# Fetch order of row names, buffers of three weight matrices, and the order of a product and a pair of transposes in a four-layer graph network

## Chip, cores and metric

The kernel runs on one core of a Trainium2 chip, as one launch. The metric is the device time of that launch in microseconds; smaller is better. Everything is in float32.

## The reference, cut to what matters

Four layers follow each other. Each one adds a graph layer over 2708 nodes of 256 features and then a feed-forward layer with routed experts to `x`. The change touches the second half of layer 1 and the start of layer 2:

```python
# layer 1, feed-forward: a shared hidden layer, then one of 8 matrices per row
H = gelu(layernorm(x) @ W1 + b1)               # 2708 x 1024
probs = softmax(H @ Wg + bg);  assign = argmax(probs)
for e in range(8):
    out += where(assign == e, probs[:, e] * (H @ Wd[e] + bd[e]), 0)
x = x + out
# layer 2, graph attention
h = layernorm(x) @ W.T
a_src = (h * attn_src).sum(-1);  a_dst = (h * attn_dst).sum(-1)
s = leaky_relu(a_src[None, :] + a_dst[:, None], 0.2), masked by adj > 0
x = x + elu(softmax(s) @ h)
```

## The kernel before

**Tiles.** Rows are worked on in 22 tiles of 128 rows (the last one has 20). `x` stays in SBUF for the whole program. The five engines are PE (matrix products and transposes), DVE and ACT (element-wise), POOL (which also starts the indirect DMAs) and SP (which starts the plain DMAs). Each engine works through its own queue in order; the framework places the waits between them and may arrange instructions of independent steps within a queue. `engine_after`, `after` and `in_order` pin an order by hand.

**Layer 1, second half.** While the graph product of a group of tiles ends, `send1` computes the hidden layer of the group and its gates, writes the hidden rows to DRAM (`hid`, line 1267) and scatters a short record for each row (its index and its weight, `taken1`, line 537), sorted by expert. Then the rows are taken up again in blocks of 128 rows that share one expert. Nine blocks (`NA`) are certain: the first two groups fill them whatever the routing of the third. Fifteen more (`ALWAYS`) take the rest.

The class `Units` runs the blocks. For a block it needs

- the names: 128 records, gathered by POOL (`fetch_names`, line 551 by way of `gather`),
- the rows: 128 hidden rows of 4 KB, gathered by POOL by those names into one of four buffers `hs` (`fetch_rows`, line 693),
- the expert's matrix, 1152 KB, loaded by SP (`weights1`, line 1170); the load is left out when the buffer already holds this expert.

PE then transposes the rows (`turn`, line 708, copied to `hTs` by ACT at line 709), multiplies (`output`, line 781), DVE adds the bias and scales (lines 784 and 785), and POOL scatters the result to DRAM (`given1`, line 537). `more` is called once per block and decides what is fetched ahead: as many rows as there are buffers, one block of names beyond that (three once all nine certain blocks have their rows), and two matrices.

**Buffers of the matrices.** `buffer_of` gives each block a buffer. The certain blocks go round three of them, in the order 0, 3, 6, 1, 4, 7, 2, 5, 8 of the sorted blocks (`in_thirds`), so that neighbours with one expert meet in one buffer. Three more lie where the gates of `send1` had their tiles (pool `w1r`, opened when the gates are closed). The rest's blocks follow the list `REST1` of (block, buffer). Ahead of block 18 stands a branch on a count that comes out as zero here (`branch`); its body recomputes blocks that hold more rows than planned.

**The turn to layer 2.** The results of tiles 0 to 7 (`EARLY`) are read back and added to `x` while the last blocks still run (line 1485); their statistics for the first two of `FOURS` (tiles 0 and 1, tiles 2 to 5) are made there too. The tiles from 8 on can be added only after the last block's scatter. Layer 2 starts by going over `FOURS`: `turned_up` adds the results (line 1587; by DVE up to tile 13, by POOL from tile 14 on) and transposes (line 1592, copied by ACT at line 1594), `valued` multiplies by the weights with two score columns (line 267), ACT takes the scores (line 1629) and exponentials, and DVE writes the scaled values (line 1632). `row_scores` and `row_factor` spread the scores over all partitions. Two of `FOURS` are prepared ahead. The third, tiles 6 to 9, is half early and half late: `finish` adds and transposes the late tiles 8 and 9 in the middle of the second four's products,

```python
if i == 2 and ahead and callable(ahead[0][2]):
    ahead[0] = (*ahead[0][:2], ahead[0][2]())
ps.append(times(xT, k, r, w_l2, D + 2, ps_acc()))
```

so that on PE two products come first, then the late transposes, then the other two products. `ps_acc` goes round five PSUM banks here, `ps_tmp` round three.

Of the kernel before, what the change touches and what calls it, by code (L numbers as in the profile page):

```python
# [8 lines left out]
F32 = mybir.dt.float32  # L9
# [57 lines left out]
def adj_ffn4(ctx: ExitStack, tc: tile.TileContext, a: dict, out: bass.AP):  # L67
# [594 lines left out]
    class Units(Blocks):  # L662
# [59 lines left out]
        def more(self, weights=True):  # L722
            while self.rows_todo and len(self.rows) < len(self.hs):
                if not self.named:
                    self.fetch_names(self.names_todo.pop(0))
                self.fetch_rows()
                self.rows_todo -= 1
            while self.names_todo and len(self.named) < (3 if self.places[1] >= self.border else 1):
                self.fetch_names(self.names_todo.pop(0))
            while weights and self.todo and len(self.ahead) < 2:  # L730
                self.fetch(self.todo.pop(0))
            if weights and not self.todo:
                self.fetch_rest()
# [142 lines left out]
    with ExitStack() as l0:  # L876
# [261 lines left out]
    ALWAYS, AHEAD1 = 15, 9  # L1138
    EARLY, prepared = GROUPS1[0], {}

    REST1 = [(0, 3), (4, 4), (6, 2), (1, 3), (5, 4), (7, 2), (2, 3), (8, 2), (3, 3),
             (9, 5), (10, 1), (11, 4), (12, 0), (14, 2), (13, 0)]

    def buffer_of(b):

        return b % 3 if b < NA else REST1[b - NA][1]

    assert sorted(b for b, _ in REST1) == list(range(ALWAYS))
    assert all(b < AHEAD1 for b, _ in REST1[:AHEAD1])
    with ExitStack() as l1:  # L1150
# [179 lines left out]
        def beside(b):  # L1330
            if b == NA + AHEAD1 + 1:
                work1.at_end = scattered["given1"][-1].name
            if b in (NA + ALWAYS - 3, NA + ALWAYS - 2):
                first = len(nc.cur_bb.bb.instructions)
                for t0 in EARLY[::2][(b - NA - ALWAYS + 3) * 2 :][:2]:
                    add_early(t0)
                engine_after(first, mybir.EngineType.DVE, work1.last)
            if b == NA + ALWAYS - 1:
                for some in FOURS[:2]:
                    prepared[some[0]] = stats(some, by_log=True)[1]  # L1340
            if b == NA + 4:
# [123 lines left out]
        def branch():  # L1465

            with tc.If(left[0] > 0):
# [48 lines left out]
    with tc.tile_pool(name="t3", reuse_waits="tile", bufs=1) as t3:  # L1516
# [34 lines left out]
        with tc.tile_pool(name="g2", reuse_waits="tile", bufs=1) as gp:  # L1551
# [17 lines left out]
            def turned_up(tiles):  # L1569

                n, t0 = len(tiles), tiles[0]
                adder = v if t0 < FOURS[4][0] else g
                xT = gp.tile([P, DC, W], F32, name="xT4", bufs=2)
                late = [t for t in tiles if t not in EARLY]
                if late:
                    o = gp.tile([P, 4, D], F32, name="mine", bufs=2)
                    for i in load_tiles(nc, o, late, given[1], t0):
                        behind(i, scattered["given1"])

                def two(k):  # L1580
                    r = rows(t0 + k + 1)
                    for q, m in (((P, 2),) if r == P else ((P, 1), (r, 1))):
                        i = k if q == P else k + 1
                        if t0 + i in EARLY:
                            continue
                        xs = x[:q, t0 + i : t0 + i + m, :]
                        adder.tensor_tensor(xs, xs, o[:q, i : i + m, :], ALU.add)
                    p = ps_tmp()
                    for i in range(2):
                        q = rows(t0 + k + i)  # L1590
                        for c in range(DC):
                            te.transpose(p[:, (c * 2 + i) * P : (c * 2 + i) * P + q],
                                         x[:q, t0 + k + i, c * P : (c + 1) * P], ident[:q, :q])
                    s.copy(xT[:, :, k * P : (k + 1) * P + r],
                           p.rearrange("p (c t) -> p c t", c=DC)[:, :, : P + r])

                def scale():
                    return prepared[t0] if t0 in prepared else stats(tiles, by_log=True)[1]

                if len(late) in (0, n):  # L1600
                    for k in range(0, n, 2):
                        two(k)
                    return tiles, xT, scale()
                for k in range(0, n - len(late), 2):
                    two(k)

                def finish():
                    had, first = last_of(fronts), len(nc.cur_bb.bb.instructions)
                    had[mybir.EngineType.DVE] = last_put[0]
                    for k in range(n - len(late), n, 2):  # L1610
                        two(k)
                    for e in fronts:
                        engine_after(first, e, had[e])
                    return None

                return tiles, xT, finish

            def valued(tiles, xT, rstd):

                n, t0 = len(tiles), tiles[0]  # L1620
                own = tiles_of(t0 * P, (n - 1) * P + rows(tiles[-1]))
                sc = gp.tile([P, 4, 2], F32, name="sc", bufs=2)
                (v if tiles in FOURS[:2] else g).memset(sc, 0.0)
                ps = []
                for i, (t, k, r) in enumerate(own):
                    if i == 2 and ahead and callable(ahead[0][2]):
                        ahead[0] = (*ahead[0][:2], ahead[0][2]())
                    ps.append(times(xT, k, r, w_l2, D + 2, ps_acc()))
                    s.activation(sc[:r, i, :], ps[-1][:, D:], AF.Copy, scale=rstd[:r, i : i + 1])
                lnexp(hh[:, t0 : t0 + n, D], sc[:, :n, 0], AF.Exp)  # L1630
                for i, (p, (t, k, r)) in enumerate(zip(ps, own)):
                    put = v.tensor_scalar(hh[:r, t, :D], p[:, :D], rstd[:r, i : i + 1],
                                          hh[:r, t, D :], op0=ALU.mult, op1=ALU.mult)
                last_put[:] = [put.ins.name]
                lnexp(G[:, t0 : t0 + n, 0], sc[:, :n, 0], AF.Exp, scale=-0.8)

                lnexp(rowe[:, t0 : t0 + n, 0], sc[:, :n, 1], AF.Exp, scale=-0.2, bias=ln8)
                return sc, t0, n

            ahead, todo = [turned_up(FOURS[0])], list(FOURS[1:])  # L1640
            for k in range(len(FOURS)):
                tiles, xT, rstd = ahead.pop(0)
                sc, t0, n = valued(tiles, xT, rstd)
                if ahead and ahead[0][2] is None:
                    ahead[0] = (*ahead[0][:2], stats(ahead[0][0], by_log=True)[1])
                had, first = {}, len(nc.cur_bb.bb.instructions)
                while todo and len(ahead) < 2:
# [640 lines left out]
```

## Time and profile before

| | us |
|---|---|
| median of 3 runs | 1890.63 (1887.06 to 1890.68) |
| the profiled execution's own time | 1905.2 |
| its span, first to last instruction | 1903.5 |
| PE busy in the span | 1822.0 |
| DVE, ACT, POOL busy | 1074.7, 656.6, 388.5 |
| blocks of layer 1, first transpose to last product | 958.7 to 1090.6 |
| first transposes of layer 2 to its first attention product | 1090.4 to 1118.9 |

The profile was taken of one execution, and its times are counted from the start of its span. A line of a timeline gives the start, the length, the engine, the line of the kernel, the operation, what is written and read, and how many instructions were merged; in brackets stands how long the engine was idle before it and what ended that. A wait's line gives who waited for whom: microseconds in total, how many times, and the longest. PE's products of float32 are recorded as two instructions each with 128-column weights. The kind "DMA_INDIRECT" on POOL is the making of the descriptors; the data land later.

### The profile page before, as it was taken

The numbers are of one execution on the slowest core, as the hardware profiler recorded it, in microseconds if no ns is written. First come the engines' busy times: TensorE is split into PE (matmuls) and PEld (weight loads), VectorE is DVE, ScalarE is ACT, GpSimd is POOL, SyncE is SP. The second block draws the span as 40 slices with busy tenths as digits, with TensorE's granted clock in tenths as the row PEclk, the third lists the DMA queues.
The fourth block names the chain that finished last, engine by engine and source line by source line (L and its number), as shares of the span: only waits on it lengthen the run. The fifth ranks groups of instructions, "written<-read, shape, count | busy, mean of one in ns | idle before, by whom it ended". The sixth has DMA issues, their size and how long they took to land. (4 is left out here: it accounts for less than half of the span.)

```text
span 1903.5 us, 25846 instructions
## 1 busy us (share of the span) xinstructions
PE 1822.0 (96%) x9453; PEld 1333.3 (70%) x9453; DVE 1074.7 (56%) x2467; ACT 656.6 (34%) x1472; POOL 388.5 (20%) x460
## 2 busy tenths in 40 slices
PE   8999998999998999999988999999899999999998
PEld 7888777888887888878777878888566733233344
DVE  7687862443433625354542265555355398888877
ACT  8877741222222302113222232222232552132232
POOL 0014353333322001403446410000000100011021
PEclk9999999999999999999999999999899999999999
DMA  8535655887773554544746541000101000012020
GB/s 263 156 105 164 227 184 212 328 330 274 284 286 105 180 153 123 128 128 129 213 139 213 172 93 20 1 1 1 44 1 34 17 1 23 23 26 37 23 37 18
DMA packets 92638, 232.81 MB, mean 122 GB/s; under 512 B 18223, under 2 KB 48983, under 8 KB 84952
## 3 DMA queue, kind: packets, MB, share of 16 engines
q1 hardware_dynamic: 70936, 184.46, 29.8%
q0 software_dynamic: 21568, 46.61, 9.0%
q8 instruction: 78, 1.28, 0.3%
q14 instruction: 56, 0.46, 0.1%
HBM read 218.39 MB, written 30.80 MB: 131 GB/s over the span
## 5 line engine op out<-in xcount | busy, mean ns | idle before, releaser
L2160 DVE SCALAR_TENSOR_TENSOR e<-arena,G,mask 128x1024 f32<-128x1024 f32 (+1 forms) x252 | 275.0, 1149 | 34.2 <-PE den L2197 33.2
L2189 PE MATMUL num<-e,wh 128*64 128x512 f32 (+4 forms) x1056 | 214.0, 549 | 0.7 <-ACT L_gnn_W L1498 0.3
L1420 PE MATMUL acc<-sup,adrow 128*128 128x256 f32 x882 | 199.9, 384 | 3.1 <-DVE adrow L1388 1.7
L1024 PE MATMUL acc<-msg,wt 128*128 128x256 f32 x882 | 199.1, 382 | 2.7 <-DVE wt L974 2.0
L1723 PE MATMUL ps_acc<-hh,e 128*128 128x257 f32 x882 | 199.2, 382 | 1.7 <-ACT o L1666 1.7
L1420 PEld LDWEIGHTS acc<-sup,adrow 128*128 128x128 f32 x882 | 166.2, 191 | 31.3 <-issue 5.5
L1024 PEld LDWEIGHTS acc<-msg,wt 128*128 128x128 f32 x882 | 165.9, 191 | 29.0 <-DVE wt L974 3.0
L1723 PEld LDWEIGHTS ps_acc<-hh,e 128*128 128x128 f32 x882 | 163.7, 190 | 29.2 <-ACT o L1666 4.2
L649 PE MATMUL yacc<-wb,hTs 128*128 128x256 f32 x736 | 170.9, 384 | 5.6 <-DVE ys L651 2.9
L615 PE MATMUL ps_acc<-xTs,wa 128*128 128x256 f32 (+1 forms) x768 | 170.3, 374 | 4.6 <-DVE xTs L605 2.6
L617 ACT ACTIVATE hTs<-ps_acc,wa 128x256 f32<-128x256 f32 (+1 forms) x192 | 88.7, 465 | 246.7 <-PE yacc L649 165.5
L615 PEld LDWEIGHTS ps_acc<-xTs,wa 128*128 128x128 f32 x768 | 136.9, 190 | 31.6 <-DVE xTs L605 5.7
L2189 PEld LDWEIGHTS num<-e,wh 128*64 128x64 f32 (+1 forms) x1056 | 70.0, 136 | 122.8 <-issue 105.0
L649 PEld LDWEIGHTS yacc<-wb,hTs 128*128 128x128 f32 x736 | 138.4, 192 | 24.9 <-DVE ys L651 4.0
L1715 DVE SCALAR_TENSOR_TENSOR e<-Rb,G,mask 128x640 f32<-128x640 f32 (+2 forms) x110 | 84.9, 773 | 90.6 <-PE ps_acc L1723 90.5
L2197 PE MATMUL den<-e,wh 128*32 128x512 f32 (+4 forms) x1056 | 112.2, 545 | 0.0
L1385 DVE TENSOR_SCALAR mask<-adrow 128x1024 uint8<-128x1024 f32 (+1 forms) x66 | 41.4, 627 | 123.8 <-DMA adrow<-in_adjT 123.2
L221 ACT COPY xT<-ps_tmp 128x256 f32<-128x256 f32 x76 | 26.8, 366 | 199.6 <-PE ps_tmp L220 199.1
L781 PE MATMUL yacc<-wb,hTs 128*128 128x256 f32 x384 | 90.9, 392 | 0.0
L974 DVE SCALAR_TENSOR_TENSOR wt<-adrow,wt 128x640 f32<-128x640 f32 (+3 forms) x67 | 71.1, 1063 | 25.7 <-ACT wt L141 24.0
L2197 PEld LDWEIGHTS den<-e,wh 128*32 128x32 f32 (+1 forms) x1056 | 33.0, 109 | 73.7 <-issue 69.6
L537 POOL DMA_INDIRECT given<-ys,xs x46 | 65.4, 1421 | 91.2 <-DVE ys L652 76.9
(487 smaller groups left out, 2626.0 us busy)
## 6 DMA issues: line engine op xcount, KB each, us to landing
adhalf<-in_adjT SPq DMA_DIRECT2D x42, 677.0 KB
wb<-in_L_ffn_W2p SPq DMA_DIRECT2D x24, 1152.0 KB
wb<-in_L_ffn_Wdp SPq DMA_DIRECT2D x24, 1152.0 KB
wa<-in_L_ffn_W1b SPq DMA_DIRECT2D x24, 1028.0 KB
adrow<-in_adjT SPq DMA_DIRECT2D x42, 512.0 KB
adrow<-in_adjT SPq DMA_DIRECT2D x42, 320.0 KB
adrow<-in_adjT SPq DMA_DIRECT2D x21, 576.0 KB
adrow<-in_adjT SPq DMA_DIRECT2D x21, 448.0 KB
```

The source lines that it names most:

```text
L615: i = te.matmul(p[:, f % 2, : m * P], lhsT=w1[:, c, f * P : (f + 1) * P], rhs=xT[:, c, : m * P], start=(c == 0), stop=(c == DC - 1))
L617: s.activation(hT[:, f, : m * P], p[:, f % 2, : m * P], AF.Gelu, bias=bias[:, f : f + 1])
L649: te.matmul(q[:, k, :], lhsT=hT[:, f, k * P : (k + 1) * P], rhs=w2[:, f, :], start=(f == 0), stop=(f == HC - 1))
L781: te.matmul(q, lhsT=hT[:, f, :], rhs=w2[:, f, :], start=(f == 0), stop=(f == HC - 1))
L974: v.scalar_tensor_tensor(wt, ad, 1.0, wt, op0=ALU.is_lt, op1=ALU.mult)
L1024: te.matmul(p[:q, n - pair[0], :], lhsT=wt[:, k : k + q], rhs=msg[:r, j, :], start=(j == 0 and n == pair[0]), stop=(j == FULL - 1 and n == ...
L1420: te.matmul(p[:q, n - pair[0], :], lhsT=ad[:, k : k + q], rhs=sup[:, jj, :], start=(jj == 0 and n == pair[0]), stop=(jj == FULL - 1 and n ...
L1715: i = v.scalar_tensor_tensor(e[:r, :w], Rb[:r, c0 : c0 + w], G[:r, j, :], mask[:r, j, c0 : c0 + w], op0=ALU.max, op1=ALU.mult)
L1723: te.matmul(p[:, : D + 1], lhsT=e[:, k : k + q], rhs=hh[:, j, :], start=(j == 0), stop=False)
L2160: v.scalar_tensor_tensor(e[:, :w], slow[:, m % 2, k, :w], G[:, j, 2 * pair + k, :], mask[:, j, c0 : c0 + w], op0=ALU.max, op1=ALU.mult)
L2189: te.matmul(num[k * DK : (k + 1) * DK, hf, :q], lhsT=wh[some, j, 2 * pair + k, :DK], rhs=e[some, :q], start=(j == 0), stop=(j == FULL), ti ...
L2197: te.matmul(den[z * Q : (z + 1) * Q, :q], lhsT=wh[some, i, 2 * pair + k, DK : DK + 1] .to_broadcast([some.stop - some.start, Q]), rhs=e[so ...
```

## The change

It has four parts.

1. `more` fetches the names of all nine certain blocks in a row, behind the first three blocks' rows, instead of one block ahead. For the rest nothing changes (up to three ahead, once the ninth block's rows are on their way).
2. `buffer_of`: the last three of the nine certain blocks (in running order 6, 7, 8) get the buffers 3, 4, 5 in the gates' room instead of 0, 1, 2. `REST1` is renamed to match: 3 becomes 0, 4 becomes 1, 2 becomes 5, 5 becomes 2, 1 becomes 4, 0 becomes 3. The branch uses buffer 0 instead of 3.
3. The statistics of tiles 6 and 7 are made beside the last two blocks, with those of tiles 0 to 5.
4. `finish` is split. `add_late` adds tiles 8 and 9 on DVE at the place where `finish` stood. The second four's products run through; then the product of tile 6 (`begin_values` up to 1), then the transposes of tiles 8 and 9 (`turn_late`), their statistics, and the products of tiles 7 to 9.

```diff
-            while self.names_todo and len(self.named) < (3 if self.places[1] >= self.border else 1):
+            while self.names_todo and (self.places[0] < self.border or
+                                       self.places[1] >= self.border and len(self.named) < 3):
                 self.fetch_names(self.names_todo.pop(0))
...
-    REST1 = [(0, 3), (4, 4), (6, 2), (1, 3), (5, 4), (7, 2), (2, 3), (8, 2), (3, 3),
-             (9, 5), (10, 1), (11, 4), (12, 0), (14, 2), (13, 0)]
+    REST1 = [(0, 0), (4, 1), (6, 5), (1, 0), (5, 1), (7, 5), (2, 0), (8, 5), (3, 0),
+             (9, 2), (10, 4), (11, 1), (12, 3), (14, 5), (13, 3)]
...
-        return b % 3 if b < NA else REST1[b - NA][1]
+        return (b % 3 if b < NA - 3 else b - NA + 6) if b < NA else REST1[b - NA][1]
...
             if b == NA + ALWAYS - 1:
-                for some in FOURS[:2]:
+                for some in (*FOURS[:2], [t for t in FOURS[2] if t in EARLY]):
                     prepared[some[0]] = stats(some, by_log=True)[1]
...
-                work1.all_again(hc, items[AHEAD1:], wbs[3][0],
+                work1.all_again(hc, items[AHEAD1:], wbs[0][0],
                                 slice(NA + AHEAD1, NA + ALWAYS))
             pin(scattered["given1"][-1].name)
-            wbs[3][1] = None
+            wbs[0][1] = None
...
-                def finish():
+                def add_late():
+                    first = len(nc.cur_bb.bb.instructions)
+                    for k in range(n - len(late), n, 2):
+                        add_two(k)
+                    engine_after(first, mybir.EngineType.DVE, last_put[0])
+
+                def turn_late():
                     had, first = last_of(fronts), len(nc.cur_bb.bb.instructions)
-                    had[mybir.EngineType.DVE] = last_put[0]
                     for k in range(n - len(late), n, 2):
-                        two(k)
+                        turn_two(k)
                     for e in fronts:
                         engine_after(first, e, had[e])
...
+            def begin_values(tiles, xT, rstd, sc, ps, upto):
+                own = tiles_of(tiles[0] * P, (len(tiles) - 1) * P + rows(tiles[-1]))
+                while len(ps) < upto:
+                    i = len(ps)
+                    t, k, r = own[i]
+                    if i == 2 and ahead and type(ahead[0][2]) is tuple:
+                        ahead[0][2][1]()
+                    ps.append(times(xT, k, r, w_l2, D + 2, ps_acc()))
+                    s.activation(sc[:r, i, :], ps[-1][:, D:], AF.Copy, scale=rstd(i, r))
+                return own
...
-                if ahead and ahead[0][2] is None:
-                    ahead[0] = (*ahead[0][:2], stats(ahead[0][0], by_log=True)[1])
                 had, first = {}, len(nc.cur_bb.bb.instructions)
+                if ahead and type(ahead[0][2]) is tuple:
+                    tiles, xT, (m, _, turn_late) = ahead[0]
+                    some = prepared[tiles[0]]
+                    begun = scores_of(tiles)
+                    begin_values(tiles, xT, lambda i, r: some[:r, i : i + 1], *begun, 1)
+                    turn_late()
+                    first = len(nc.cur_bb.bb.instructions)
+                    others = stats(tiles[m:], by_log=True)[1]
+                    engine_after(first, mybir.EngineType.DVE, last_put[0])
...
+                    ahead[0] = (tiles, xT, rstd, begun)
+                    begin_values(tiles, xT, rstd, *begun, len(tiles))
+                    had, first = last_of(fronts), len(nc.cur_bb.bb.instructions)
```

Outside the lines shown, `two` is split into `add_two` and `turn_two`, `valued` into `scores_of`, `begin_values` and the rest, and the scale is passed as a function of the tile.

More of the change, by code (lines that the diff above doesn't have):

```diff
@@ L1578, in turned_up, with add_two @@
                         behind(i, scattered["given1"])
-                def two(k):
+                def add_two(k):
                     r = rows(t0 + k + 1)
@@ L1587, in two, with turn_two @@
                         adder.tensor_tensor(xs, xs, o[:q, i : i + m, :], ALU.add)
+                def turn_two(k):
+                    r = rows(t0 + k + 1)
                     p = ps_tmp()
@@ L1598, in scale @@
                     return prepared[t0] if t0 in prepared else stats(tiles, by_log=True)[1]
+                for k in range(0, n if len(late) == n else n - len(late), 2):
+                    add_two(k)
+                    turn_two(k)
                 if len(late) in (0, n):
-                    for k in range(0, n, 2):
-                        two(k)
-                    return tiles, xT, scale()
-                for k in range(0, n - len(late), 2):
-                    two(k)
-                def finish():
+                    rstd = scale()
+                    return tiles, xT, lambda i, r: rstd[:r, i : i + 1]
@@ L1608, in finish @@
+                def add_late():
+                    first = len(nc.cur_bb.bb.instructions)
+                    for k in range(n - len(late), n, 2):
+                        add_two(k)
+                    engine_after(first, mybir.EngineType.DVE, last_put[0])
+                def turn_late():
                     had, first = last_of(fronts), len(nc.cur_bb.bb.instructions)
-                    had[mybir.EngineType.DVE] = last_put[0]
                     for k in range(n - len(late), n, 2):
-                        two(k)
+                        turn_two(k)
@@ L1612, in finish @@
                     for e in fronts:
                         engine_after(first, e, had[e])
-                    return None
-                return tiles, xT, finish
-            def valued(tiles, xT, rstd):
-                n, t0 = len(tiles), tiles[0]
[L1621 to L1629, printed above, removed]
+                return tiles, xT, (n - len(late), add_late, turn_late)
@@ new lines, in scores_of @@
+            def scores_of(tiles):
+                sc = gp.tile([P, 4, 2], F32, name="sc", bufs=2)
+                (v if tiles[0] < FOURS[2][0] else g).memset(sc, 0.0)
+                return sc, []
+            def begin_values(tiles, xT, rstd, sc, ps, upto):
[8 more added lines that the diff above has]
+                return own
@@ L1630, in valued @@
+            def valued(tiles, xT, rstd, begun=None):
+                n, t0 = len(tiles), tiles[0]
+                sc, ps = begun or scores_of(tiles)
+                own = begin_values(tiles, xT, rstd, sc, ps, n)
                 lnexp(hh[:, t0 : t0 + n, D], sc[:, :n, 0], AF.Exp)
                 for i, (p, (t, k, r)) in enumerate(zip(ps, own)):
-                    put = v.tensor_scalar(hh[:r, t, :D], p[:, :D], rstd[:r, i : i + 1],
-                                          hh[:r, t, D :], op0=ALU.mult, op1=ALU.mult)
+                    put = v.tensor_scalar(hh[:r, t, :D], p[:, :D], rstd(i, r), hh[:r, t, D :],
+                                          op0=ALU.mult, op1=ALU.mult)
@@ L1641, in adj_ffn4, with rstd @@
             for k in range(len(FOURS)):
-                tiles, xT, rstd = ahead.pop(0)
-                sc, t0, n = valued(tiles, xT, rstd)
-                if ahead and ahead[0][2] is None:
-                    ahead[0] = (*ahead[0][:2], stats(ahead[0][0], by_log=True)[1])
+                sc, t0, n = valued(*ahead.pop(0))
                 had, first = {}, len(nc.cur_bb.bb.instructions)
+                if ahead and type(ahead[0][2]) is tuple:
[7 more added lines that the diff above has]
+                    engine_after(first, mybir.EngineType.DVE, last_put[0])
+                    def rstd(i, r):
+                        return some[:r, i : i + 1] if i < m else others[:r, i - m : i - m + 1]
+                    ahead[0] = (tiles, xT, rstd, begun)
+                    begin_values(tiles, xT, rstd, *begun, len(tiles))
+                    had, first = last_of(fronts), len(nc.cur_bb.bb.instructions)
                 while todo and len(ahead) < 2:
```

## The prediction, made before the changed kernel was run

> **What bounds the kernel now.** I read the page first, then PE's waits, then the busy time by stage over layer 1's second half (the stage that the change touches), then the timelines of PE, POOL and SP there. TensorE is busy for 96% of the span, so an edit can win only where PE stands still, or where it runs slowly after standing still.
>
> ```profile
> PE 1822.0 (96%) x9453; PEld 1333.3 (70%) x9453; DVE 1074.7 (56%) x2467; ACT 656.6 (34%) x1472; POOL 388.5 (20%) x460
> ```
>
> Four of PE's longer single waits in the whole program lie inside the 160 us concerned (total, times, longest):
>
> ```profile
> PE ps_acc L708 <- ACT hTs L709: 6.9, 1, 6.9
> ...
> PE ps_acc L708 <- PEq L1467: 3.6, 1, 3.6
> ...
> PE ps_acc L708 <- DMA hs<-hid,names: 3.3, 1, 3.3
> ...
> PE ps_tmp L1592 <- DVE x L1587: 2.4, 1, 2.4
> ```
>
> By stage (PE busy, PEld, DVE, ACT, POOL, clock, DMA share, GB/s): PE loses 6.7 of 17 us with the DMA engines mostly idle, then 4.5 of 23 us with them full. POOL is the busiest after PE.
>
> ```profile
> 978.00:995.00 17.00, 10.28 (x46) 9.13 (x47) 3.79 (x17) 2.83 (x5) 9.87 (x10) 0.80 0.32 94
> 995.00:1018.00 23.00, 18.51 (x97) 15.84 (x96) 2.71 (x7) 3.92 (x7) 14.49 (x15) 0.95 0.94 360
> ```
>
> Call the stalls A (977.8 to 984.7) and B (1011.7 to 1016.7). Timeline lines of both:
>
> ```profile
> 984.08 1.07 ACT L709 COPY hTs<-ps_acc 128x512 f32<-128x512 f32 x2 [10.35 <-remote]
> ...
> 984.72 1.97 PE L708 MATMUL ps_acc<-ident,hs 128*128 128x128 f32 x8 [6.95 <-ACT hTs L709]
> ...
> 1003.27 1.04 POOL L693 DMA_INDIRECT hs<-hid,names  x1 [0.30 <-PE ps_acc L708]
> ...
> 1015.05 0.63 PE L708 MATMUL ps_acc<-ident,hs 128*128 128x128 f32 x4 [3.35 <-DMA hs<-hid,names]
> ...
> 1016.70 1.11 PE L708 MATMUL ps_acc<-ident,hs 128*128 128x128 f32 x4 [1.02 <-issue]
> 1017.60 6.05 PE L781 MATMUL yacc<-wb,hTs 128*128 128x256 f32 x16
> ```
>
> B is read directly: counted in order, the gather of hidden rows issued at 1003.27 is the eleventh, and PE's eleventh set of turns waits until 1015.05 for it, 11.8 us. A gather with idle DMA engines (issued 965.50) has its last packet at 969.6: 4.1 us. Stall A ends on a copy of ACT whose own releaser the trace does not show ("remote"); DVE's and SP's instructions are held in the same microseconds. I can't name its cause.
>
> What holds the gathers back is on POOL's queue and SP's:
>
> ```profile
> 961.39 1.00 POOL L551 DMA_INDIRECT names<-taken,b_ix  x1 [0.31 <-issue]
> ...
> 965.50 1.04 POOL L693 DMA_INDIRECT hs<-hid,names  x1 [3.11 <-DMA names<-taken,b_ix]
> ...
> 991.54 0.37 SPq L1170 DMA_DIRECT2D wb<-in_L_ffn_Wdp  x1
> 994.99 5.14 SPq L1170 DMA_DIRECT2D wb<-in_L_ffn_Wdp  x3
> ```
>
> The names of one block are fetched only one block ahead, so POOL issues names, waits for them to land, then issues the rows (4.1 us from issue to issue). And the weights of blocks 6, 7, 8 (matrices of 1152 KB) wait for blocks 3, 4, 5 to give their buffers back: SP issues them from 991.5 to 998.9, the first two of the rest at 999.9 and 1001.4, and the packets of 9216 bytes run until 1013.9, right over the gathers of blocks 9 to 11. Blocks 3, 4, 5 load nothing (their experts are in the buffers already; those issues last under 0.1 us, without packets).
>
> **What the skill says.** *DMA: Bandwidth & Descriptors*, "Issuing engines are not separate DMA queues": what SP and POOL start runs on the same 16 engines and interleaves. The trace agrees: the same gather takes 4.1 us alone and 11.8 us beside weight loads. *Perfetto Trace Analysis*, "DMA Instruction — SWDGE (GPSIMD)": the profiled end of a POOL DMA is that of its descriptors, not of the data; here 1.04 us against 4.1. *TensorE: Matmul & The Clock Gate*, Part 1: after an idle window of about 3.4 us PE runs at half clock until it has been busy as long. The trace agrees: 16 matmuls take 6.05 us behind stall B, 3.62 us elsewhere.
>
> **The change part by part.**
>
> *Names in a row.* POOL issues 1.31 us apart. At the start of the certain blocks six name gathers stand behind the first three rows instead of one: 929.7 + 6 x 1.31 = 937.6. Queued behind them are a memset (932.3 now) and the fourth row gather (934.97 now), each about 4 us later: landing at 944 becomes about 948, and PE turns that block at 972. Cost nothing. Further on, four name gathers leave POOL between 961 and 988 (5.2 us of its queue) and four waits for names go. The fifth gather onwards then waits for its buffer only; the eighth still stands behind the six scatters of line 537 (their order is kept), so it moves from 984.4 to some 981; the ninth from 991.2 to about 986; the names of the rest, behind it, from 992.5 to about 987. The rest's gathers start some 5 us earlier.
>
> *Three matrices in the closed gates' room.* The count of loads stays: 6, 7, 8 load before and after; the rest's buffers are renamed so that each takes over the same expert as before, and its first two load into 0 and 1 as they did into 3 and 4. What moves is the time. SP is through with block 5's skipped load at 980.2 (it waits for block 2's output) and takes 0.9 us per issue, so 6, 7, 8 go at about 981, 982, 983 if the room is free; the last reader of the gates' tiles that I find ends at 977.0 (line 494). The rest's two wait for blocks 3 and 4: 991.5 and 995. So 3.5 MB go into a stretch with 94 GB/s, and out of the one with 360 GB/s. No PE wait on a weight exists now, so this alone wins nothing directly; it clears the way for gathers 10 to 12.
>
> *Sum of layer 1.* Stall B costs 3.35 + 1.02 idle, and 6.05 - 3.62 + 1.11 - 0.60 = 2.9 of slow clock: 7.3 us. Next late is POOL: three issues per block, 3.9 us, against 4.33 us of PE per block, so it keeps up with little to spare. The upper end is 7.3; the lower end 2, since what shows in one execution need not be as long in those timed; I take 5. Stall A (6.95 idle + 0.93 + 0.95 slow = 8.8 us) stays in my forecast: neither part removes anything that I can tie to it.
>
> *Layer 2.* Now PE has done two of the second four's products at 1096.1 and stands until 1098.57 for the sum of tiles 8 and 9 (chain: last scatter 1091.7, its landing, the load at 1094.7, DVE at 1097.7). Afterwards the other two products and one of the next four's come first, 3 x 0.87 = 2.6 us, more than the stall of 2.42. What is next late: the product of tile 7 needs a PSUM bank that DVE frees only at about 1099.5 (some 0.1 to 0.4 us), and the turns of tiles 14 to 17 need POOL's sums, which end at 1104.86, on a load (1098.45) that hangs on the same sum of 8 and 9 and doesn't move. Those turns start at 1105.64 now and end at 1106.5; they could then end at 1105.3. So 1.2 us of 2.42 is kept. Bounds: 2.4 won; 1 lost, if the scores of tiles 8 and 9, which now wait for their own statistics, hold back copies behind them on ACT. The statistics of tiles 6 and 7 move beside the last two blocks: two pairs at 0.37 + 0.17, 1.1 us on DVE from 1086.7. They delay line 784 (1087.17) by 0.6 us; its scatter stands behind POOL's constant loads until 1089.3 anyway: nothing.
>
> *Sum.* 5 + 1.2 = 6.2 us. The profiled execution took 1905.2 us (span 1903.5), 14.6 more than the median 1890.63: 1905.2 becomes about 1899, and the median 1884.4.
>
> **The rivals.** *Unsure cover (same)*: stalls A and B look like part of the 14.6 us that the profiled execution takes more. Then only layer 2 is won, 1889.4. For it: what ends A is not seen; against: B ends on a plain transfer beside a full DMA. *Stall A goes too (faster)*: POOL's queue is 5.2 us shorter just there; if names and rows in that queue are what holds A, 8.8 us more go: 1875.6. *The burst hits the gathers (slower)*: if A is absent when timed, PE turns block 7 at about 990, and the weights of 6, 7, 8 and of the rest's first two come in one burst from 981. The eighth gather, issued at 981.6, then takes 11.8 instead of 4.1 us and lands at 993.4: PE stands 3.4 us and pays 2.9 of slow clock, 6.3 in all, less 1.2: 1895.7, if nothing was to be won at B. It decides if the gather takes more than 8.4 us. For it: 11.8 was seen. Against: gathers are four buffers deep and only one is so close.
>
> **How the numbers follow.** About 0.2% (3.8 us) can be told from no change. Forecast 0.48 (1882 to 1886.8), A too 0.12, unsure cover 0.26, burst 0.14. Faster 0.60, same 0.26, slower 0.14. The predicted time is the first's, 1884.4. The range leaves out the burst and some of the case where all of A goes: 1876 to 1891.5.
>
> **What would show it.** Right: nine name gathers ahead of 940 on POOL and none between 960 and 985; SP's real weight issues near 981 to 983; no DMA wait of line 708 behind block 9, and a DMA share near 0.7 or less in 995 to 1018; no PE wait on L1587. Wrong: those issues still after 990 (the room is freed late), a PE wait on hs at block 7 or 8, a wait of L267 on DVE's line for hh, or the turns of tiles 14 to 17 no earlier against the end of layer 1.

## The result, and the profile after

| | us |
|---|---|
| before, median of 10 runs beside the changed kernel | 1888.80 (1884.76 to 1891.11) |
| changed, median of 10 runs | 1882.53 (1879.08 to 1888.05) |
| ratio | 0.9972 (0.9959 to 0.9986) |
| profiled execution of the changed kernel, own time and span | 1882.29, 1880.6 |
| blocks of layer 1, first transpose to layer 2's first | 118.4 (before 131.7) |
| layer 2's first transpose to its first attention product (its "start" from here on) | 32.5 (before 28.5) |

In brackets behind a ratio stands its 95% interval. By the ratio the changed kernel is 0.28% faster, 5.3 us of 1888.8; the two medians lie 6.3 us apart. The forecast was 6.2 us. One thing has to be known before the two profiles are laid side by side. The experiments ran on three chips, and the kernel before took 1885.8, 1904.7 and 1904.5 us on them (medians of 48 to 60 runs). The profile of before (1905.2) looks like the two slower chips in its time and in its stalls, that of after (1882.29) like the faster one; which chip either came from is not on record. So 131.7 against 118.4 most likely compares two chips as well as two kernels.

PE's and the other engines' busy time, and then PE's longest waits from the first block to the first attention product of the changed kernel (total, times, longest):

```profile
PE 1820.4 (97%) x9453; PEld 1335.0 (71%) x9453; DVE 1076.1 (57%) x2468; ACT 656.0 (35%) x1474; POOL 387.3 (21%) x460
```

```profile
PE ps_acc L708 <- DMA hs<-hid,names: 3.8, 4, 2.3
PE ps_tmp L1596 <- ACT xT L1598: 3.4, 1, 3.4
PE ps_acc L708 <- PEq L1468: 2.1, 1, 2.1
```

The 6.9 us on ACT's copies and the 2.4 us on DVE's sum are gone. A wait that was not there, on a copy in layer 2, is the longest single one. By stage (PE busy, PEld, DVE, ACT, POOL, clock, DMA share, GB/s), with the first blocks 14 us earlier than in the profile of before:

```profile
964.00:981.00 17.00, 15.65 (x79) 13.33 (x79) 3.70 (x12) 3.41 (x6) 7.13 (x7) 1.00 0.96 350
...
981.00:1004.00 23.00, 20.56 (x107) 17.75 (x106) 3.12 (x8) 5.09 (x10) 15.93 (x16) 0.93 0.59 192
```

The full DMA engines have moved to the stage where they were mostly idle. In stall B's stage PE loses 2.4 of 23 us instead of 4.5, at a DMA share of 0.59 instead of 0.94. One stop is still there, 2.26 us for the rows of the 11th block, the very block of stall B:

```profile
992.25 1.39 PE L708 MATMUL ps_acc<-ident,hs 128*128 128x128 f32 x8 [2.26 <-DMA hs<-hid,names]
```

POOL's queue in the changed kernel (start, length, operation, idle before it):

```profile
918.55 1.01 POOL L551 DMA_INDIRECT names<-taken,b_ix  x1 [0.31 <-issue]
...
925.16 1.20 POOL L551 DMA_INDIRECT names<-taken,b_ix  x1 [0.30 <-issue]
926.37 0.96 POOL L1450 MEMSET hs<- 128x1024 f32 x1
927.60 1.01 POOL L693 DMA_INDIRECT hs<-hid,names  x1 [0.27 <-POOL hs L1450]
...
972.36 1.05 POOL L551 DMA_INDIRECT names<-taken,b_ix  x1 [3.39 <-DVE ys L786]
973.72 1.01 POOL L551 DMA_INDIRECT names<-taken,b_ix  x1 [0.31 <-issue]
975.04 1.00 POOL L551 DMA_INDIRECT names<-taken,b_ix  x1 [0.30 <-DMA wb<-in_L_ffn_Wdp]
983.49 1.00 POOL L693 DMA_INDIRECT hs<-hid,names  x1 [7.44 <-issue]
```

All nine names are out by 926.4. The names of the rest leave from 972.4 on, and the next rows only at 983.5: between them lie 11 us, where names and rows stood 4.1 us apart before. SP's eight issues of the stage, three of them without packets, are one line; the five loads' packets of 9216 bytes run from 964.0 to 985.2:

```profile
959.58 12.24 SPq L1171 DMA_DIRECT2D wb<-in_L_ffn_Wdp  x8
```

The plain DMAs of the whole program are 144 packets and 1.18 MB fewer (section 3 of the page; before, then after):

```profile
q1 hardware_dynamic: 70936, 184.46, 29.8%
```

```profile
q1 hardware_dynamic: 70792, 183.28, 29.8%
```

That is one matrix. It was not foreseen: with the new names block 9 of the rest finds its expert in buffer 2, which the old order had overwritten with the ninth certain block's.

### The profile page after: what moved, and what is told of

Same layout as the page of the kernel before. It is cut to its first block, busy times and chain, and to the rows that moved or that the text cites. A ratio compares the mean times of both kernels' runs of the same rounds, so it can differ in the third digit from the quotient of the medians.

```text
span 1880.6 us, 25848 instructions
## 1 busy us (share of the span) xinstructions
PE 1820.4 (97%) x9453; PEld 1335.0 (71%) x9453; DVE 1076.1 (57%) x2468; ACT 656.0 (35%) x1474; POOL 387.3 (21%) x460
## 5 line engine op out<-in xcount | busy, mean ns | idle before, releaser
L1025 PEld LDWEIGHTS acc<-msg,wt 128*128 128x128 f32 x882 | 165.5, 191 | 26.7 <-DVE wt L975 1.8
L1386 DVE TENSOR_SCALAR mask<-adrow 128x1024 uint8<-128x1024 f32 (+1 forms) x66 | 41.6, 630 | 124.1 <-DMA adrow<-in_adjT 123.7
L221 ACT COPY xT<-ps_tmp 128x256 f32<-128x256 f32 x76 | 26.8, 366 | 199.1 <-PE ps_tmp L220 198.7
```

What stands on the lines that cost most here:

```text
L1025: te.matmul(p[:q, n - pair[0], :], lhsT=wt[:, k : k + q], rhs=msg[:r, j, :], start=(j == 0 and n == pair[0]), stop=(j == FULL - 1 and n == ...
```

## The experiments

The theory after this reading: layer 1 wins more than the total, by names that are out of the way and by one load less, and layer 2 loses through the new wait on ACT. The rival is the prediction's own sum (5 in layer 1, 1.2 in layer 2). Runs 1 to 4 shared a chip (the faster one), 5 to 8 a second, 9 to 12 a third; each ratio is to the kernel before on the same chip.

The table is counted from each trace: start of the first transposes of some blocks, in us after those of block 1, and of layer 2's first transposes. PE comes to the branch ahead of the 20th block's transposes. Blocks are counted from 1 here; where the section on the change and some forecasts count from 0, "the stops at blocks 7 and 8" are those of the 8th and 9th block here.

| profile | 7 | 8 | 9 | 10 | 12 | 19 | 20 | 21 | layer 2 |
|---|---|---|---|---|---|---|---|---|---|
| layer 2 alone (first chip) | 18.9 | 33.8 | 44.2 | 51.1 | 59.1 | 87.2 | 99.6 | 106.2 | 127.0 |
| layer 1 alone (first chip) | 18.9 | 30.7 | 35.9 | 43.0 | 52.3 | 80.7 | 90.9 | 95.3 | 116.2 |
| changed | 18.9 | 31.0 | 36.2 | 43.5 | 53.7 | 81.5 | 91.6 | 97.6 | 118.4 |
| before | 26.9 | 39.5 | 43.9 | 51.1 | 64.8 | 93.6 | 105.1 | 111.0 | 131.7 |
| names alone (second chip) | 23.7 | 36.3 | 40.6 | 49.0 | 55.1 | 89.3 | 101.1 | 107.1 | 127.9 |
| names alone (third chip) | 24.5 | 38.2 | 42.5 | 50.5 | 56.6 | 84.3 | 94.0 | 98.4 | 120.6 |
| buffers alone (second chip) | 26.8 | 39.2 | 45.2 | 52.1 | 60.5 | 97.5 | 108.4 | 115.7 | 136.4 |
| buffers alone (third chip) | 26.1 | 39.4 | 44.9 | 51.9 | 59.9 | 99.1 | 110.2 | 114.6 | 135.3 |
| one buffer (second chip) | 26.7 | 39.5 | 43.9 | 50.8 | 62.9 | 91.0 | 99.3 | 103.7 | 128.5 |
| names and one buffer (second chip) | 23.6 | 37.6 | 42.0 | 49.2 | 55.3 | 83.1 | 95.3 | 102.4 | 123.1 |
| changed again (third chip) | 24.6 | 38.2 | 42.5 | 49.4 | 58.0 | 86.3 | 94.8 | 99.2 | 124.1 |

**1. Layer 1 alone.** The kernel before with parts 1 and 2 of the diff as they stand in the section on the change.

> The kernel before with the names in a row and the renamed buffers alone; layer 2 stays as before. Theory of the prediction (layer 1 wins 5, layer 2 another 1.2): 4.5 to 5 us under the kernel before, ratio about 0.9974. Rival, from the two profiles (the blocks stage became 13.4 us shorter, layer 2's start 4.0 us longer): this kernel is the faster of the two, 8 to 13 us under before, ratio 0.993 to 0.996, and its profile has 28.5 us between the first turn of layer 2 and its first attention product. A third, that layer 1 wins nothing outside the one profiled execution: ratio 1.000.

Measured: 1881.62, ratio 0.9974 (0.9963 to 0.9984), 4.9 us won. The size is the prediction's. The rival's 8 to 13 us, read off the two profiles, are excluded, and with them its 28.5 us: layer 2's start took 30.8.

**2. Layer 2 alone.** The changed kernel with parts 1 and 2 taken back.

> The kernel before with the layer-2 parts alone (statistics of tiles 6 and 7 early, product of tile 6 ahead of the late turns). Prediction: 1.2 us won, ratio 0.9994 (bounds: 2.4 won to 1 lost). Rival, from the profile after: ACT's exponential of the spread scores of tiles 0 and 1 stands ahead of the score of tile 7 and the copies, waits 4.3 us for its DMA and stops PE for 3.4 us: 2 to 4 us lost, ratio 1.001 to 1.002, and the profile shows a wait of the transposes' bank on ACT's copy and 32 us from the first turn to the first attention product.

Measured: 1887.60, ratio 1.001 (0.9999 to 1.0021). The point lies on the rival's side, the interval reaches from 0.2 us won to 4 lost, and the predicted 1.2 us won lies outside it. The stop that the rival named did not come: with layer 1 as before, ACT stood 2.49 us for the same DMA, and PE stopped 1.63 us, on POOL's sum of tiles 14 and 15. The start of layer 2 took 29.5 us.

This run is also the only profile of the old layer 1 on the faster chip. It has no stall A (block 7 starts at 18.9) and little of stall B (0.91 us at the 11th block). PE's timeline of layer 2 alone at blocks 8, 9 and behind the branch, then of layer 1 alone at blocks 8, 9, 11 and behind the branch:

```profile
980.05 1.94 PE L708 MATMUL ps_acc<-ident,hs 128*128 128x128 f32 x8 [3.48 <-DMA hs<-hid,names]
981.79 5.54 PE L781 MATMUL yacc<-wb,hTs 128*128 128x256 f32 x16
990.41 1.07 PE L708 MATMUL ps_acc<-ident,hs 128*128 128x128 f32 x8 [3.08 <-DMA hs<-hid,names]
...
1045.83 1.94 PE L708 MATMUL ps_acc<-ident,hs 128*128 128x128 f32 x8 [4.38 <-PEq L1467]
1047.57 5.08 PE L781 MATMUL yacc<-wb,hTs 128*128 128x256 f32 x16
```

```profile
979.02 1.06 PE L708 MATMUL ps_acc<-ident,hs 128*128 128x128 f32 x8 [0.40 <-DMA hs<-hid,names]
979.92 3.62 PE L782 MATMUL yacc<-wb,hTs 128*128 128x256 f32 x16
984.21 1.06 PE L708 MATMUL ps_acc<-ident,hs 128*128 128x128 f32 x8 [0.67 <-DMA hs<-hid,names]
...
995.41 1.06 PE L708 MATMUL ps_acc<-ident,hs 128*128 128x128 f32 x8 [2.17 <-DMA hs<-hid,names]
...
1039.25 1.06 PE L708 MATMUL ps_acc<-ident,hs 128*128 128x128 f32 x8 [2.28 <-PEq L1468]
1040.15 3.62 PE L782 MATMUL yacc<-wb,hTs 128*128 128x256 f32 x16
```

Both old stops, at blocks 8 and 9, end on rows, with half clock behind the first (eight transposes take 1.94 instead of 1.06 us): 3.48 + 3.08 idle, 1.94 - 1.06 and 5.54 - 3.62 slow, 9.4 us, against 0.40 + 0.67. That is the 8.3 us that the table shows up to block 9. The stop at the 11th block is longer than before, 2.17 against 0.91, and gives 1.4 back by block 12. At the branch 4.38 + 0.88 + 1.46 stand against 2.28: 4.4 us more. The blocks of this pair differ by 10.8 us, but layer 1 alone began its blocks 2.1 us later and spent 1.3 more at layer 2's start, which leaves 7.4; the medians differ by 6.0.

**3. The exponential later.** In the changed kernel, part of the loop over `FOURS`:

```diff
-                row_factor(Rb[:, t0 * P : (t0 + n) * P], kept, 0, t0, n)
+                if k == 1:
+                    begin = len(nc.cur_bb.bb.instructions)
+                    had = last_of((mybir.EngineType.Activation,))
+                    lnexp(Rb[:, : t0 * P], Rb[:, : t0 * P], AF.Exp, scale=0.8)
+                    engine_after(begin, mybir.EngineType.Activation,
+                                 had[mybir.EngineType.Activation])
+                if k == 0:
+                    row_read(Rb[:, t0 * P : (t0 + n) * P], kept, 0, t0, n)
+                else:
+                    row_factor(Rb[:, t0 * P : (t0 + n) * P], kept, 0, t0, n)
```

> The changed kernel with one ACT instruction moved: the exponential over the spread scores of tiles 0 and 1 stands behind the copies of tiles 10 to 13, where the kernel before had it. If that instruction's wait is what stops PE at 1076 in the profile after: the 3.36 us go at least in part, and what is late next is POOL's sum of tiles 14 and 15 (ends at 1077.7, 1.7 us after PE runs dry at 1075.97); 1.6 us plus some of the half-clock time, 2 to 3 us under the changed kernel, ratio to before about 0.9955. If the late sums or the statistics are the cause instead: the same time as the changed kernel, 0.997.

Measured: 1880.61, ratio 0.9971 (0.9961 to 0.9980). ACT in the changed kernel, where the exponential (line 141) waits for the spread scores and three scores and two copies stand behind it; then PE there, and PE with the exponential moved:

```profile
1071.89 0.58 ACT L1598 COPY xT<-ps_tmp 128x512 f32<-128x512 f32 x1 [0.31 <-PE ps_tmp L1596]
1076.76 0.42 ACT L141 ACTIVATE Rb<-Rb 128x256 f32<-128x256 f32 x1 [4.29 <-DMA Rb<-rows]
1077.09 0.24 ACT L1639 ACTIVATE sc<-ps_acc,var 128x2 f32<-128x2 f32 x1
...
1078.63 1.05 ACT L1598 COPY xT<-ps_tmp 128x512 f32<-128x512 f32 x2
```

```profile
1075.70 0.27 PE L1497 MATMUL ps_tmp<-ident,sc 128*4 128x128 f32 x1
1079.33 1.09 PE L1596 MATMUL ps_tmp<-ident,x 128*128 128x128 f32 x4 [3.36 <-ACT xT L1598]
```

```profile
1075.67 0.27 PE L1497 MATMUL ps_tmp<-ident,sc 128*4 128x128 f32 x1
1077.74 0.66 PE L1596 MATMUL ps_tmp<-ident,x 128*128 128x128 f32 x4 [1.79 <-POOL x L1588]
```

The cause of the new wait is shown: the stop becomes 1.79 us, its end is POOL's sum at the time that was expected, the clock stays full, and layer 2's start shrinks from 32.5 to 30.5 us. In the time nothing can be told from the changed kernel (expected 0.9955); 2 us are 0.1%, as much as the interval to either side.

**4. And three buffers for the results read back.** As run 3, with `name="mine", bufs=3`.

> The kernel with the exponential moved, and three buffers instead of two for the results read back, so that the load of tiles 14 to 17 need not wait for the sum of 8 and 9. If POOL's sums are what is late next (their load went out at 1071.2 and landed at 1076.4), they start some 3 us sooner and PE has no stop left in layer 2's start: about 1.7 us under the kernel with the exponential moved alone, ratio to before about 0.9945. If the load is not the limit: the same as that kernel.

Measured: 1880.66, ratio 0.9976 (0.9965 to 0.9988): the same as run 3. In the profile two stops of 1.31 (on DVE's sum) and 1.10 us (on POOL's) remain, and the start took 29.2 us. So the load was one limit, with another 1 us behind it, and the time shows neither.

**5. Names alone.** Part 1 of the diff.

> The kernel before with the nine certain blocks' names fetched in a row, nothing else. By the prediction (the order of names and rows on POOL is what is won, the weights only clear the way): most of layer 1's 5 us, ratio 0.998 or less, and no DMA wait of line 708 at blocks 7 and 8. Rival, from the profiles of the first experiments: the renamed buffers save one weight load (two real loads stand ahead of the branch where the old buffers are, one where the new are), and with it PE's stop at the branch falls from 4.4 us and 2.3 of half clock to 2.2: then this kernel keeps the long stop at the branch and wins only the stops of blocks 7 and 8, some 2 to 3 us, ratio 0.9985.

Measured on the second chip: 1900.97, ratio 0.9983 (0.9971 to 0.9995), 3.2 us won. The interval holds both forecasts; the long stop at the branch is kept (3.83 us), as the rival had it. No wait on rows stands at blocks 8 and 9, but the profile of before has none there either; what is gone against that profile is stall B (blocks 9 to 12 take 14.5 us instead of 20.9). A matrix now comes late (1.27 us, line 782).

**6. Buffers alone.** Part 2 of the diff.

> The kernel before with the renamed buffers alone; names one block ahead as before. By the prediction: nothing won directly, and five loads in a row ahead of names and rows that are fetched late: 1.000 or slower. Rival (one load less, shorter stop at the branch): 2 to 4.4 us won, ratio 0.998 to 0.9985, PE's stop at the branch near 2.2 us, but the stops at blocks 7 and 8 still there, as long as or longer than 3.5 and 3.1.

Measured: 1916.66, ratio 1.0062 (1.0046 to 1.0079), 11.8 us lost. That is slower, as the prediction's side had it without a size; the rival is excluded. Where the 11.8 us go is only in part the burst: the profile has a stop of 5.38 us in the middle of the 12th block's transposes, and layer 2's start takes 31.4 us instead of 28.5.

**7. One buffer.** The kernel before with

```diff
-        return b % 3 if b < NA else REST1[b - NA][1]
+        return (b % 3 if b < NA - 1 else 5) if b < NA else REST1[b - NA][1]
```

and 2 and 5 exchanged in `REST1`.

> The kernel before with only the ninth certain block's matrix in the gates' room (buffer 5), the other buffers as before: one weight load less behind it, the other loads where they were, no burst of five. If the load ahead of the branch is what makes PE's stop there long: stop near 2.2 us instead of 4.4, no half clock behind it, 3 to 4.4 us won, ratio 0.998. If the stop at the branch has another cause: 3.5 to 4.4 us as before, ratio 1.000.

Measured: 1908.22, ratio 1.0016 (1.0003 to 1.0029): slower, though the stop at the branch was gone in its profile (0.33 us; 8.3 us from block 19 to 20, where before has 11.5). Both cases missed. Its profile loses the time at the turn to layer 2. There the last scatter of layer 1 leaves 3.67 us behind layer 2's first transposes (which begin at 1089.20) instead of 1.30, PE stops 4.88 us for DVE's sum instead of 2.42, and layer 2's start takes 32.3 us instead of 28.5:

```profile
1092.87 1.04 POOL L537 DMA_INDIRECT given<-xn,names  x1 [0.30 <-issue]
```

```profile
1099.80 1.08 PE L1592 MATMUL ps_tmp<-ident,x 128*128 128x128 f32 x4 [4.88 <-DVE x L1587]
```

Every kernel with matrices in the gates' room has some of this, run 12 apart. The last scatter leaves 1.30 us behind the first transposes in before and in runs 2, 5 and 10; 2.26 to 2.60 in the changed kernel and in runs 1, 3, 4, 6, 9 and 11; 3.67 and 3.94 in runs 7 and 8. With the old buffers POOL has issued all seven constant loads of layer 2 ahead of the last two scatters. With the renamed ones the first of them comes later and stands between these two, in runs 7 and 8 the other six do. That the loads wait for room which the last matrices now hold is likely, but not shown. The prediction counted none of it.

**8. Names and one buffer.** Runs 5 and 7 together.

> The kernel before with the names in a row and only the ninth certain block's matrix in the gates' room. If the burst of five loads costs the changed kernel what it shows at the tenth block (names of the rest land after 10 us, PE stops 2.2 us there): this one is 2 us faster than layer 1's parts together, ratio 0.996. If the loads are better early (they then lie over the gathers of blocks 9 to 11 again): no faster than layer 1's parts together, 0.9974 or more, with DMA waits of line 708 from block 9 on.

Measured: 1904.06, ratio 1.0001 (0.9984 to 1.0018). The time is the second case's, without the waits on rows that it named; layer 2's start took 33.0 us, as in run 7. The stop at the branch was 4.26 us with one load less, as in run 7, so the number of loads alone does not decide it. On the faster chip four profiles with one load had 2.1 to 2.3 us and the single one with two had 4.4.

The traces tell more about this stop. PE's branch is on record with its length in ns, 5.4 us in run 1 and 7.4 us in run 2:

```profile
L1468 PEldq COMPARE_BRANCH  x1: 5352/5352/5352, 1033.6 to 1033.6; - x1
```

```profile
L1467 PEldq COMPARE_BRANCH  x1: 7392/7392/7392, 1038.1 to 1038.1; - x1
```

In all fourteen profiles PE goes on 1.7 to 1.9 us after a DMA packet of the kind "instruction" (16 KB) has landed, the first one behind PE's branch. That packet starts 1.0 us after the branch where no packet of a matrix is under way (runs 7 and 9: stops of 0.33 and 0.51 us), 2.0 to 3.9 us after it where one matrix is, and 4.2 to 5.0 us where two are (before, runs 2 and 5). Runs 1 and 2 have 2.98 and 5.03 us, and their stops differ by the same 2.1 us. So what counts seems to be not how many loads there are, but whether their packets are under way between PE's branch and this packet: in run 8 the one load went out 1.0 us after the branch, and the packet started 3.8 us after it. The order and the lengths agree in every profile; no run moved this packet alone.

**9. The changed kernel again**, on the third chip.

> The changed kernel once more, for its stages on the chip that runs the next three. If the two parts of layer 1 help each other (names out of the way before the five loads come): 0.997 to 0.9975 here too, though the names alone gave 0.9983 and the buffers alone 1.0062 where they were measured. If each part has its own effect and they add: 1.003 to 1.004 on a chip where stall A shows.

Measured: 1907.43 against 1904.47, ratio 1.0016 (1.0002 to 1.0030), between the two cases. On this chip the changed kernel is slower. Its profile does not show why: from block 1 to layer 2's first attention product it takes 154.5 us, before's 160.2, but it begins its blocks 4.5 us later. Stall A is there (4.79 us), in the middle of the 6th block's transposes ("turns"), and so is a second stop in the middle of the 11th block's:

```profile
986.80 1.97 PE L708 MATMUL ps_acc<-ident,hs 128*128 128x128 f32 x8 [4.79 <-ACT hTs L709]
...
1014.29 0.60 PE L708 MATMUL ps_acc<-ident,hs 128*128 128x128 f32 x4
1017.24 0.66 PE L708 MATMUL ps_acc<-ident,hs 128*128 128x128 f32 x4 [2.35 <-issue]
```

**10. Names alone, 11. buffers alone**, beside run 9.

> Names in a row alone, beside the changed kernel on one chip. If the names carry layer 1's gain: within 0.001 of the changed kernel. If the buffers bring their share once the names are out of the way (one load and the long stop at the branch less): 0.001 to 0.002 above it, with the stop at the branch between 3.5 and 4.4 us where the changed kernel has 2.2.

> The renamed buffers alone, beside the changed kernel on one chip. Five loads in a row from the sixth block on, over names that are fetched one block ahead: the names of blocks 7 to 10 and their rows land late, and PE stops for them. Slower than before wherever it is measured, 1.004 to 1.007. If that was a matter of one chip: 0.998 to 1.000 here.

Measured: names 1902.05, ratio 0.9996 (0.9980 to 1.0011); buffers 1915.05, ratio 1.0056 (1.0038 to 1.0074). The names' cases both missed: alone they are 0.2% faster than the changed kernel here, and the stop at the branch is 1.75 us against 0.51. The buffers lose 10.7 us on a second chip, as forecast, so that was no accident; 4.2 us more than in before stand in layer 2's start there (32.7 us). The single parts of layer 1 add up to 1.0052 and the whole change, layer 2 included, is 1.0016: 0.36% less, with some 0.28% of uncertainty on that difference. The parts help each other, as run 9's first case had it, but on this chip the sum is still a loss. Past block 10, stops in mid-turn of 5.38 (run 6) and 5.24 us (run 11) stand in the buffers' profiles, 2.35 in run 9, 4.30 in run 12, and none in the three profiles (5, 8, 10) with names in a row in which the 7th and 8th block's matrices load into their old buffers, later.

**12. The exponential later, and the constant load behind the last scatter.** As run 3, with

```diff
-                tc.add_manual_dep(i, work1.at_end, mybir.DependencyInfo(
+                tc.add_manual_dep(i, scattered["given1"][-1].name, mybir.DependencyInfo(
```

> The changed kernel with the exponential moved as in the earlier run, and POOL's first constant load of layer 2 behind the last scatter of layer 1 (it stands ahead of it, and waits 2.4 us for its room). If that load holds the last scatter back: the scatter goes about 1.0 us sooner after the last product, and so do the sums of tiles 8 to 17; layer 2's start, 30.5 us in the run with the exponential moved alone, becomes 29 to 29.5, ratio 0.0005 under the changed kernel with the exponential moved. If the scatter waits for DVE instead: no change.

Measured: 1908.12, ratio 1.0016 (1.0000 to 1.0032). POOL at the end of layer 1 in run 9, then in run 12:

```profile
1088.44 0.76 POOL L127 DMA_DIRECT2D L_ffn_Wr<-in_L_ffn_Wr  x1 [2.38 <-issue]
1089.50 1.02 POOL L537 DMA_INDIRECT given<-xn,names  x1 [0.30 <-issue]
```

```profile
1090.68 0.98 POOL L537 DMA_INDIRECT given<-xn,names  x1 [2.47 <-DVE sc L1628]
1091.66 0.78 POOL L127 DMA_DIRECT2D L_ffn_Wr<-in_L_ffn_Wr  x1
```

Layer 2's first transposes began at 1087.24 and 1089.39, so the scatter left 2.26 and 1.29 us behind them: the 1.0 us that was expected. The order on POOL is what does it, for with the exponential moved alone (run 3) the scatter left 2.27 us behind. Layer 2's start went from 30.4 to 29.9 us, the moved exponential included. The time is that of run 9.

## Why the prediction was right, and where it was not

**The size of layer 1** (5 us) was right on one chip: 4.9 in run 1. **Its place was not, there.** The working put it at stall B, the rows of the 11th block. On the faster chip B is 0.91 us, and the change makes it longer (2.17): the rows of block 10 wait on POOL for names that are held up by the loads, and those of block 11 stand behind them. What the change removes there is the wait of blocks 8 and 9 for rows that were late because of the names. In the profiles of the slower chips, to which the profile of before seems to belong, B does go: blocks 9 to 12 take 20.9 us in before, 13.3 to 15.5 with names in a row (runs 5, 8, 9 and 10), and 15.3 and 15.0 with the buffers alone, which lose more elsewhere. But the time won there is 3.2 and 0.8 us with the names alone, and 3 us are lost with the whole change. That the sum fits is in good part luck.

The mechanism named for the queue on POOL was the right one. The eighth gather of rows stands directly behind the six scatters, as worked out, and leaves 19.4 us after block 1 began (22.3 forecast, 25.7 before; 19.3 to 19.7 in every kernel with names in a row). Of the signs of being right one failed, besides the times of the loads: a wait on rows stands behind block 9, 2.26 us at the 11th. Two signs of being wrong were seen: short waits on rows at the 8th and 9th block (0.70 and 0.65 us), and the transposes of tiles 14 to 17, which begin 16.4 us behind layer 2's first instead of 15.2.

**"Cost nothing" for the six names ahead of the fourth row** held in the blocks: that row left at 927.6, and nothing waited for it. Whether they cost something ahead of the blocks is open. On the slower chips the kernels with names in a row begin block 1 at 961.4 to 964.2 us, the others at 958.0 to 962.5.

**"The count of loads stays"** failed: one load went. What it is worth in time is not settled; in the profiles it shortens the stop at the branch where its packets were under way there (run 8). **The times of the loads** came earlier than forecast (18.4 to 20.6 us after block 1 began instead of 22.3 to 24.3), since the forecast carried stall A along; with stall A, in run 9, they are 21.4 to 24.3.

**Stall A stays** was assumed, and the changed kernel's profile has none. That is the chip, not the change: the old layer 1 has none on the faster chip, and all eight profiles of the slower chips have it. There the kernels with names in a row begin block 7 at 23.6 to 24.6 us and the others at 26.1 to 26.8, so about 2.5 us of it go with the names. The rival "A goes too" had that much right. The rival "unsure cover" was right that A need not be there in the timed runs, and wrong that layer 1 then wins nothing. A seems not to be most of the 14.6 us by which the profile exceeded the runs: against run 2's, the profile of before is 14.5 us longer, and 12.4 of that lie ahead of block 1.

What holds ACT's copy in stall A can be read further than the prediction had it. The copy waits for PE's own signal (a semaphore update) that four transposes are done. In all five profiles of the faster kind each of PE's 46 such signals stands 0.01 to 0.02 us behind the end of its transposes. In the profile of before the transposes end at 976.90 and 977.34 (the profile models the ends), the signals behind them are on record at 984.00 and 984.07, and the copy starts at 984.08, 7.2 us after the first end. In the mid-turn stop of run 9 four of PE's signals come in a bunch, from 1016.53 to 1016.70, for work that ended between 1013.15 and 1014.89. So A and the stops in mid-turn look like one thing, late signals, on the slower chips alone. Why they are late stays open; some signals are missing from these traces.

**The burst** is real. On the faster chip it costs some 1.3 us at the 11th block, since names issued at 975.8 in run 1 let the rows behind them go only at 986.9. It was forecast for the eighth gather, which escaped because its names were already there. The rival's sign, above before, was met on the third chip (1.0016), but not by its mechanism. With names left late the new buffers cost 0.6%; that the burst makes the mid-turn stops there is argued, not shown, and in the profiles 2.9 and 4.2 us of the loss lie in layer 2's start. *DMA: Bandwidth & Descriptors* of the Trainium skill, "Issuing engines are not separate DMA queues", says that such transfers interleave on the same engines, and the 11 us agree. It does not explain stops without a transfer at their end.

**Layer 2, 1.2 us won,** failed: run 2 has 0.2 won to 4 lost. The wait on DVE's sum went as worked out in the changed kernel, and POOL's sum of tiles 14 and 15, which was named as next late, was so in runs 2, 3, 4 and 12. Left out was that with the new order of products the exponential of tiles 0 and 1 stands ahead of the scores and copies on ACT, where it waits for a DMA issued at 1073.0 that lands at 1076.7. Also left out was that the renamed buffers put a constant load of layer 2 ahead of the last scatter, which then leaves 1.0 us later (run 12). The lower bound (1 us lost, copies held back on ACT) had the right engine. So the total was hit by a layer 1 of the right size at another place, and a layer 2 too small to be told from nothing.

## What to carry to other kernels

Small gathers that something waits for go ahead of a row of large loads; the new buffers alone, which move the loads into idle DMA time, made this kernel 0.6% slower, and with the gathers out of the way the whole change cost a third of that on the same chip and won on another. When buffers are renamed, read the queues at the next stage too: here loads of layer 2's constants came later, and the last scatter behind them left 1.0 to 2.6 us later. When an edit changes the order of products, read every engine's new queue for an instruction that waits for a DMA: one exponential held three scores and two copies. A change of 0.3% has to be timed on more than one chip before it is called a gain.

## What the runs showed of the hardware that was not expected

- Three chips gave 1885.8, 1904.7 and 1904.5 us for one kernel, 1% apart, and 0.9972 and 1.0016 for the same change.
- On the slower chips PE stops 4 to 7 us in the transposes of blocks 6 and 7 in every profile; on the faster one in none. PE's signal to ACT, 0.01 to 0.02 us behind the transposes in every case on the faster chip, comes up to 7 us late there.
- PE went on behind its branch 1.7 to 1.9 us after a 16 KB packet of the kind "instruction" had landed, in all fourteen profiles. The packet started 1.0 us after the branch with no matrix packets under way, up to 5.0 us after it with two matrices.
- Two profiles of the same kernel on two of the slower chips (runs 5 and 10) differ by 7.4 us in the blocks. A stage of one profile there settles nothing below that.
- A stop of PE of 3.08 us (block 9) was followed by full clock (run 2: 1.07 us for eight transposes), one of 2.83 us by half clock (run 6, at the branch: 1.94 us), so the length of a stop alone did not tell, and the window of about 3.4 us that the prediction draws on does not decide between these two.
